# A cross-attention block on one core: an fc pair's weight sums made behind the exchange's copies, batch 1's spread rows loaded later, and batch 3's output projection by seven products of quarter blocks

## The chip, the cores and the metric

The kernel runs on one core of a Trainium2 chip. The metric is the time of one execution on the device in microseconds (us). Engines are called as in the profile: PE multiplies matrices (PEld loads its weights), DVE is the vector engine, ACT the scalar engine, POOL GpSimd, and SP the engine whose queue issues most of the transfers. Each engine works through its own instructions in the order in which they were written, and waits at semaphores for the others.

## The reference, cut to what matters

Four batches of 512 rows by 512 columns, 16 heads of 32 columns, all in float32:

```python
x = layer_norm(hidden_states, ln1_w, ln1_b)
q = (x @ q_w + q_b)...;  k = (enc @ k_w + k_b)...;  v = (enc @ v_w + v_b)...
scores = where(mask, einsum('bhqd,bhkd->bhqk', q, k) / sqrt(32), finfo.min)
out = einsum('bhqk,bhkd->bhqd', softmax(scores), v)
hidden = out @ cproj_w + cproj_b + hidden_states
y = gelu(layer_norm(hidden, ln2_w, ln2_b) @ fc_w + fc_b)     # 512 -> 2048
return hidden + y @ proj_w + proj_b                          # 2048 -> 512
```

The output projection that the change rewrites is `out @ cproj_w` of the last batch.

## The kernel before

**Attention in 32 half-blocks.** Sixteen steps `w` (batch `w // 4`, head group `w % 4` of four heads) have two halves each, so half-blocks p = 0 to 31. `block` computes scores for two query tiles of 128 rows (`scores`, L317), takes minimum and exponential (`soften`, L323 on DVE and L327 on ACT), and turns the probabilities with 32x32 transposes on DVE (`turn`, L335) into a tile `tb`. The exchange (`copies`) then regroups `tb` across partitions into `pT` (for some half-blocks into the free space of `gt` or `xe`): four copies on POOL (L393) for the diagonal pieces and twelve transfers on SP's queue (L398) for the others. `attend` (L415, tiles `av`) multiplies the result with the values and writes `oT`. There is one `pT`, so the next exchange can begin only when `attend` has read the last one. `attend(p - 2)` stands at the start of half-block p from p = 10 on.

**Fill work.** Between the softmax steps PE gets other products: projections of later steps (`acck`, `accq`, `accv`), the output projection of a finished batch (`cproj`, tiles `accc`, L455), and the MLP of batches 0 and 1 (`fc_by_pair`, tiles `q…`, L576; `proj`, tiles `accp`, L636). A table of `put(p, ...)` calls writes by hand which piece stands in which half-block; `some(n)` takes the next n pieces of the MLP list. Nothing is scheduled by a planner: the written order is the order on each engine.

**Seven products.** A pair of fc weight blocks is multiplied with seven products of half-size blocks instead of eight (the Strassen-Winograd scheme). It needs four sums of the weights; `fc_sums` makes them on POOL (`a_sums`, L527 and L530) for up to two pairs ahead, into the two slots of `wsum`, and for batch 0's pairs stores them to `ws` in DRAM with two transfers of POOL's own queue (L619, L620), for batches 2 and 3 to load again (`load_wa`). Before, `fc_sums` is called at the end of `fc_by_pair` and `proj`, right after those have put PE's work in.

**Batch 1's layer norm** comes as rows: `store_rn` writes scale and offset to DRAM, `load_rn` (L213) loads them spread over all partitions (tiles `rn`), `ln1_rows` applies them on POOL (L218), `ln1_affine` on ACT (L222). `load_enc(1)` (L179) brings the next encoder block into `xe`.

**The stretch after the last half-block.** It is written out at the end of `xattn_block`: `attend(15, 0)`, four last pieces of the MLP of batch 1 (`accp_1_0` to `accp_1_3`), `attend(15, 1)`, batch 3's `cproj` for four row tiles, and the weight sums `p_sums`; then `last_mlps` runs the MLPs of the rest, all by seven or 49 products. PSUM has eight banks; `acc_tile` hands them out in turn, four from each of two pools.

```python
run(mlp + norm(2, 2, 3))
p_sums(first_c)
load_wa(first_c + 1)
c = C(B - 1)
run(c[:2])
p_sums(first_c + 2)
run(c[2:])
```

Of the kernel before, what the change touches and what calls it, by code (L numbers as in the profile page):

```python
# [12 lines left out]
F32 = mybir.dt.float32  # L13
# [38 lines left out]
def xattn_block(ctx: ExitStack, tc: tile.TileContext, x, rawT, encT, mask, q_w, k_w, v_w, c_w, fc_w, p_w, vecs, rows, out):  # L52
# [124 lines left out]
    def load_enc(b):  # L177
        for d in range(ND):
            queue(b).dma_start(out=eT[:, d, :], in_=encT[b, ts(d, P), :])  # L179
# [30 lines left out]
    def load_rn(b):  # L210
        S["rows", b] = [hids.tile([P, L], F32, tag="hid2", bufs=2, name=f"rn_{b}_{i}") for i in range(2)]
        for i in range(2):
            nc.sync.dma_start(out=S["rows", b][i], in_=S["rn", b][i : i + 1, :].broadcast_to([P, L]))  # L213

    def ln1_rows(b, *ds):
        for d in ds:
            for i, op in enumerate((ALU.mult, ALU.add)):
                nc.gpsimd.tensor_tensor(S["xn", b][d], S["xn", b][d], S["rows", b][i], op)  # L218

    def ln1_affine(b):  # L220
        for d in range(ND):
            nc.scalar.activation(  # L222
                xT[:, d, :], S["xn", b][d], AF.Identity,
                bias=vec[:, LN1B + d : LN1B + d + 1], scale=vec[:, LN1W + d : LN1W + d + 1],
            )
# [34 lines left out]
    def prep_q(w):  # L260
        b, g = divmod(w, NG)
        qT = k_q(w, 1)
        parts = [slice(0, L)] if w else [slice(0, 2 * P), slice(2 * P, L)]
        for c in parts:
            acc = acc_tile(f"accq_{w}_{c.start}")[:, c]
            for d in range(ND):
                nc.tensor.matmul(acc, S["wq", w][:, d, :], xT[:, d, c], start=(d == 0), stop=(d == ND - 1))  # L267
            nc.scalar.activation(qT[:, c], acc, AF.Identity, bias=qb[:, g : g + 1], scale=-scale)
        load_w(w + 2, names=("wq",))
        S["qT", w] = qT  # L270

    def prep_v(w):
        b = w // NG
        v = five.tile([P, NT, P], F32, tag="v", name=f"v_{w}")
        acc = acc_tile(f"accv_{w}")
        for t in range(NT):
            for d in range(ND):
                nc.tensor.matmul(  # L278
                    acc[:, ts(t, P)], eT[:, d, ts(t, P)], S["wv", w][:, d, :],
                    start=(d == 0), stop=(d == ND - 1),  # L280
                )
        load_w(w + 2, names=("wv",))
        nc.scalar.copy(v, acc.rearrange("p (t f) -> p t f", t=NT))
        S["v", w] = v
        if w:
            v_bias(w)
# [114 lines left out]
    def attend(w, half):  # L401

        b, g = divmod(w, NG)
        if g == 0 and half == 0:
            S["oT", b] = one.tile([P, NG, L], F32, tag="oT", name=f"oT_{b}")
        v, pT = S["v", w], S["pT", w, half]
        av = acc_tile(f"av_{w}_{half}")
        o = S["oT", b][:, g, ts(half, 2 * P)]
        shape, kw = "p (a i q) -> p a i q", dict(a=2, i=NI)
        pv = pT[:, :, :PW].rearrange("p i (a t h q) -> p t h a i q", a=2, t=NT, h=HG)  # L410
        p = [[pv[:, t, h] for h in range(HG)] for t in range(NT)]
        r = pT[:, :, PW:].rearrange("p i (a q) -> p a i q", a=2)
        for t in range(NT):
            for h in range(HG):
                nc.tensor.matmul(  # L415
                    av[ts(h, HD), : 2 * P].rearrange(shape, **kw), v[:, t, ts(h, HD)], p[t][h],
                    start=(t == 0), stop=(t == NT - 1),
                )
        o, a = o.rearrange(shape, **kw), av[:, : 2 * P].rearrange(shape, **kw)
        nc.vector.tensor_tensor(o, a, r, ALU.mult)  # L420
        del held[target(w, half)]
        exchange()
# [28 lines left out]
    def cproj(b, t):  # L451
# [5 lines left out]
        if not stays(b, t):  # L457
            (nc.sync if b == B - 1 else nc.gpsimd).dma_start(out=S["xa", b][ts(t, P), :], in_=h)

    def load_xn(b):  # L460

        for t in range(NT):
            S["h", b, t] = tiles.tile([P, D], F32, tag="xn", name=f"hn_{b}_{t}")
            Q[0].dma_start(out=S["h", b, t], in_=S["xa", b][ts(t, P), :])
# [144 lines left out]
    def fc_sums():  # L609

        while count[3] < len(fc_pairs) and count[3] < count[4] + 2:
            b, c = fc_pairs[count[3]]
            if ("fcw", b, 2 * c + 1) not in S:
                return
            x, y = raw_pair(b, c)
            s = wsum[:, count[3] % 2]
            a_sums(x[:, :2], x[:, 2:], y[:, :2], y[:, 2:], s[:, 0], s[:, 1], y[:, :2], s[:, 2], nc.gpsimd)
            if b == 0:
                nc.gpsimd.dma_start(out=sums_dram[c, :, :3], in_=s)  # L619
                nc.gpsimd.dma_start(out=sums_dram[c, :, 3], in_=y[:, :2])  # L620
            S["ws", b, c] = s[:, 0], s[:, 1], y[:, :2], s[:, 2]
            count[3] += 1

    def fc_by_pair(b, c):
        q, k = divmod(2 * c, FQ)
        fc_seven(b, c, gT[q % 2][:, k : k + 2, :], raw_pair(b, c), S["ws", b, c], acc_half, q % 2)
        count[1] += 2
        count[4] += 1
        load_mlp()
        fc_sums()  # L630

    def proj(b, q, t):
        gelus(q % 2)
        acc = acc_tile(f"accp_{b}_{q}_{t}")
        for k in range(FQ):
            nc.tensor.matmul(  # L636
                acc, gT[q % 2][:, k, ts(t, P)], S["pw", b, q * FQ + k], start=(k == 0), stop=(k == FQ - 1)
            )
        h = S["hid", b, t]
        nc.vector.tensor_tensor(h, acc, h, ALU.add)  # L640
        if q == NQ - 1:
            (nc.gpsimd if b == 0 else nc.sync).dma_start(out=out[b, ts(t, P), :], in_=h)
        count[1] += 1
        load_mlp()
        fc_sums()

# [20 lines left out]
    def last_mlps():  # L669
        last, = pools(ctx, last=1)  # L670
        ps_last = banks.pop()
        assert count[5] % 8 < 4
        count[5] = 0
        ga = last.tile([P, NP, 2, L], F32, tag="ga", name="ga")
        gs = last.tile([P, 3, NP, HL], F32, tag="gs", name="gs")
# [226 lines left out]
    def do(fn):  # L902
        return [(0.0, fn)]

    def next_(fn):
        return [(0.01, fn)]
# [13 lines left out]
    def C(b):  # L920
        return [(CHAIN, lambda t=t: cproj(b, t)) for t in range(NT)]
# [11 lines left out]
    def run(work, budget=None):  # L933

        spent = 0.0
        while work and (budget is None or spent + work[0][0] / 2 <= budget):
            cost, fn = work.pop(0)
            fn()
            spent += cost
        return spent  # L940
# [45 lines left out]
    def some(n):  # L986
        taken = []
        while n > 0:
            n -= 1 if mlp[0][0] == CHAIN else 2
            taken.append(mlp.pop(0))  # L990
        assert n == 0
        return taken
# [4 lines left out]
    def h_(b, *ts_):  # L997
        return do(lambda: load_h(b, *ts_))

    def cb(b):  # L1000
        return do(lambda: c_bias(b))
# [4 lines left out]
    def rs(b):  # L1006
        return do(lambda: ln_rs((2, b)))

    def stat(b, *ts_):
        return do(lambda: [stat2(b, t) for t in ts_])  # L1010
# [6 lines left out]
    def put(p, *work, before=(), mid=()):  # L1017

        work = [item for part in work for item in part]
        ahead[p], mids[p] = list(before), list(mid)  # L1020
        fills[p] = work
# [4 lines left out]
    k5, q5, v5 = A(5)  # L1026
    k6, q6, v6 = A(6)
    put(0, [(CHAIN, lambda: prep_v(1)), v2], do(lambda: store_rn(1)), [k2])
    put(1, [k3, (0.0, lambda: prep_q(1)), (CHAIN, lambda: (prep_v(3), load_enc(1), load_rn(1)))])
    put(2, [q2], [k4], do(lambda: ln1_rows(1, 0, 1)))  # L1030
    put(3, [q3, v4], do(lambda: ln1_rows(1, 2, 3)))
    put(4, [k5, v5], do(lambda: ln1_affine(1)))
    put(5, [q4, q5])
    put(6, [k6, q6])
# [18 lines left out]
        do(lambda: load_rn(3)), some(1))  # L1053

    k, q, v = A(11)
    put(16, do(lambda: ln1_rows(3, *range(ND))), [k, q], some(2))
    put(17, h_(1, 0, 1), next_(lambda: ln1_affine(3)), h_(1, 2, 3), x4, cb(1), C(1))
    k, q, v = A(12)
    put(18, [q], some(2), [k])
    k, q, v = A(13)  # L1060
# [20 lines left out]
    for p in range(2 * NW):  # L1081
        w, half = divmod(p, 2)
        if half == 0 and w and w % NG == 0:
            make_mb(w // NG)
        run(ahead[p])
        for pair in due.get(p, ()):
            attend(*divmod(pair, 2))

        def fill(n, work=fills[p]):
            if n or not work or work[0][0] <= CHAIN:  # L1090
                run(work, CHAIN if n < 2 else None)

        block(w, half, fill, any(cost > CHAIN for cost, _ in fills[p]), mids[p])
# [3 lines left out]
    load_h(B - 1, *range(NT))  # L1097
    run(stat(2, 0, 1))
    attend(NW - 1, 0)
    run(some(2) + stat(2, 2, 3) + rs(2) + cb(B - 1) + norm(2, 0, 1) + some(2))  # L1100
    load_wa(first_c)
    attend(NW - 1, 1)
    run(mlp + norm(2, 2, 3))
    p_sums(first_c)
    load_wa(first_c + 1)
    c = C(B - 1)
    run(c[:2])
    p_sums(first_c + 2)
    run(c[2:])
    att.close()  # L1110
    last_mlps()

# [44 lines left out]
```

## Time and profile before

| | |
|---|---|
| runs | 767.69, 768.56 and 765.34 us, median 767.69 |
| the profiled execution | 765.46 us, of which 763.7 us are its span |
| PE busy | 757.0 us |
| DVE, ACT, POOL busy | 591.2, 336.5 and 329.3 us |
| granted TensorE clock | 1.0 |

A page of the profile shows one execution. Rows of a timeline give the start and the length in microseconds, the engine, the line of the kernel, the operation, and the tiles (output<-input); in brackets stands how long the engine had been idle before it and what ended that. Matmuls of float32 are recorded twice each, so that one written matmul is two records. They overlap by their latency, so the rate of PE is read from start to start, not from a record's length.

### The profile page before, as it was taken

How to read it: one execution, taken by the hardware profiler on the slowest of the kernel's cores; microseconds unless marked ns; L12 is line 12 of the kernel's file. 1: busy time of each engine (PE TensorE's matmuls, PEld its weight loads, DVE VectorE, ACT ScalarE, POOL GpSimd, SP SyncE). 2: the span in 40 equal slices, each digit the busy share in tenths (PEclk: the TensorE clock that was granted, in tenths of full speed). 3: DMA queues.
4: the chain of work that ended last, by engine and by line, in shares of the span. 5: the costliest groups of instructions: out<-in, count | busy, mean ns of one | idle time of the engine just before them, and what ended most of it. 6: DMA issues, size and time to landing. Idle time of an engine off the chain costs nothing.

```text
span 763.7 us, 12836 instructions
## 1 busy us (share of the span) xinstructions
PE 757.0 (99%) x4346; PEld 512.8 (67%) x4346; DVE 591.2 (77%) x1186; ACT 336.5 (44%) x765; POOL 329.3 (43%) x347
## 2 busy tenths in 40 slices
PE   9999999999999999999999999999999999999998
PEld 7655455566574545475454566447888889988997
DVE  3888999879895777887887989855777886747862
ACT  2566766565773574637753567401202221022200
POOL 1538647368564874244575534430050014303152
PEclk9999999999999999999999999999999999999999
DMA  8999879467876686665756867783724402146001
GB/s 328 334 250 243 218 202 258 109 204 210 249 222 212 171 251 198 163 181 125 179 133 186 214 202 187 172 291 131 268 98 135 163 27 90 35 135 217 1 15 42
DMA packets 60576, 134.58 MB, mean 176 GB/s; under 512 B 11312, under 2 KB 17072, under 8 KB 60384
## 3 DMA queue, kind: packets, MB, share of 16 engines
q1 hardware_dynamic: 58448, 126.73, 57.3%
q0 software_dynamic: 1920, 7.01, 2.8%
q8 instruction: 35, 0.57, 0.3%
q14 instruction: 29, 0.24, 0.1%
q10 hardware_dynamic: 144, 0.02, 0.0%
HBM read 69.23 MB, written 11.02 MB: 105 GB/s over the span
## 4 chain that ended last, share of the span: by engine, by line
PE 93%; DMA 4%; SPq 2%; DVE 1%; issue 0%; POOL 0%; POOLq 0%
PE q L576 24%; PE accp L636 11%; PE r L723 8%; PE av L415 8%; PE accc L455 7%; PE sc L317 7%; PE acck L255 7%; PE accq L267 6%; PE accv L278 3%; PE accv L298 3%; PE q4p L759 2%; PE q1p L777 2%; SPq L398 2%; PE tp L166 1%; DMA pbt<-fc_w_dram 1%; DMA ptt<-v_w_dram 1%
## 5 line engine op out<-in xcount | busy, mean ns | idle before, releaser
L327 ACT ACTIVATE ptt<-ptt,mn 128x512 f32<-128x512 f32 x256 | 181.6, 711 | 143.0 <-DVE mn L323 142.9
L323 DVE CUSTOM_DVE_ANT_0 ptt<-sc,mb 128x512 f32<-128x512 f32 x256 | 160.6, 682 | 19.3 <-PE sc L317 19.2
L335 DVE STREAM_TRANSPOSE tb<-ptt 128x1024 f32<-128x1024 f32 x128 | 153.3, 1217 | 0.0
L393 POOL COPY pT<-tb 32x1088 f32<-32x1088 f32 x96 | 104.7, 1090 | 58.8 <-DMA pbt<-p_w_dram 19.0
L636 PE MATMUL accp<-pbt,gt 128*128 128x512 f32 x192 | 84.8, 595 | 0.0
L576 PE MATMUL q<-yT,gt 128*128 128x256 f32 x320 | 78.9, 379 | 0.0
L597 ACT ACTIVATE ga<-ga,vec 128x512 f32<-128x512 f32 x40 | 26.7, 714 | 92.3 <-DVE ga L530 92.3
L576 PEld LDWEIGHTS q<-yT,gt 128*128 128x128 f32 x320 | 60.8, 190 | 8.7 <-issue 0.2
L636 PEld LDWEIGHTS accp<-pbt,gt 128*128 128x128 f32 x192 | 35.9, 190 | 45.1 <-issue 39.9
L317 PE MATMUL sc<-pbt 32*128 32x512 f32 x512 | 65.3, 614 | 0.0
L576 PE MATMUL q<-ys,gt 128*128 128x256 f32 x240 | 61.6, 379 | 0.0
L255 PE MATMUL acck<-xe,ptt 128*128 128x512 f32 x128 | 58.5, 600 | 0.7 <-DVE tb L335 0.7
L267 PE MATMUL accq<-xe,ptt 128*128 128x512 f32 (+1 forms) x136 | 58.5, 574 | 0.0
L455 PE MATMUL accc<-wc,oT 128*128 128x512 f32 x128 | 56.5, 597 | 0.0
L530 DVE TENSOR_TENSOR ga<-q,ga 128x512 f32<-128x512 f32 (+1 forms) x60 | 36.2, 603 | 21.8 <-PE q L576 20.0
L576 PEld LDWEIGHTS q<-ys,gt 128*128 128x128 f32 x240 | 45.6, 190 | 6.2
L327 ACT ACTIVATION_READ_ACCUMULATOR ptt<-ptt,mn 128x1 f32 x256 | 47.8, 187 | 0.0
L415 PE MATMUL av<-pT,v 128*32 128x256 f32 x768 | 46.4, 382 | 1.4 <-DMA pT<-tb 0.7
L267 PEld LDWEIGHTS accq<-xe,ptt 128*128 128x128 f32 x136 | 24.9, 190 | 31.4 <-issue 22.5
L455 PEld LDWEIGHTS accc<-wc,oT 128*128 128x128 f32 x128 | 23.8, 190 | 31.6 <-issue 27.2
L255 PEld LDWEIGHTS acck<-xe,ptt 128*128 128x128 f32 x128 | 23.4, 191 | 31.6 <-issue 22.2
L317 PEld LDWEIGHTS sc<-pbt 32*128 32x128 f32 x512 | 27.3, 183 | 24.9 <-issue 15.8
(190 smaller groups left out, 1228.4 us busy)
## 6 DMA issues: line engine op xcount, KB each, us to landing
pT<-tb SPq DMA_DIRECT2D x288, 136.0 KB, 2.4
pbt<-p_w_dram SPq DMA_DIRECT2D x40, 256.0 KB, 3.8
gt<-ws SPq DMA_DIRECT2D x20, 512.0 KB, 3.4
gt<-tb SPq DMA_DIRECT2D x48, 136.0 KB, 4.3
xe<-tb SPq DMA_DIRECT2D x48, 136.0 KB, 2.8
pbt<-fc_w_dram SPq DMA_DIRECT2D x24, 256.0 KB, 3.5
gt<-fc_w_dram SPq DMA_DIRECT2D x20, 256.0 KB, 3.3
ptt<-k_w_dram SPq DMA_DIRECT2D x16, 256.0 KB, 3.3
```

What stands on the lines that cost most here:

```text
L255: nc.tensor.matmul(acc, S["wk", w][:, d, :], eT[:, d, :], start=(d == 0), stop=(d == ND - 1))
L267: nc.tensor.matmul(acc, S["wq", w][:, d, :], xT[:, d, c], start=(d == 0), stop=(d == ND - 1))
L317: nc.tensor.matmul(S["sc", w, qt][h], qT[r, ts(qt, P)], kT[r, :], start=True, stop=True)
L323: nc.vector.tensor_tensor_reduce(out=s, in0=S["sc", w, qt][h], in1=S["mb", w // NG], scale=1.0, scalar=FMAX, op0=ALU.add, op1=ALU.min, acc ...
L327: nc.scalar.activation(s, s, AF.Exp, bias=mn, scale=-1.0, accum_out=S["sums", w][:, qt, h : h + 1])
L335: nc.vector.transpose(tv[:, qt % 2, 2 * k : 2 * k + 2], S["ps", w, qt, k])
L393: nc.gpsimd.tensor_copy(pT[ts(i, HD), i], tb[ts(i, HD), i])
L415: nc.tensor.matmul(av[ts(h, HD), : 2 * P].rearrange(shape, **kw), v[:, t, ts(h, HD)], p[t][h], start=(t == 0), stop=(t == NT - 1),)
L455: nc.tensor.matmul(acc, S["oT", b][:, g, ts(t, P)], wc[:, g, :], start=(g == 0), stop=(g == NG - 1))
L576: nc.tensor.matmul(o, x[:, k], y[:, k], start=(k == 0), stop=(k == 1))
L636: nc.tensor.matmul(acc, gT[q % 2][:, k, ts(t, P)], S["pw", b, q * FQ + k], start=(k == 0), stop=(k == FQ - 1))
L723: nc.tensor.matmul(r, x[:, c], w[:, c], start=(c == 0), stop=(c == NP // 2 - 1))
```

## The change

It has four parts:

1. `fc_sums` is no longer called in `fc_by_pair` and `proj`, but once in each half-block from p = 11 on, after `attend` (which issues the copies of a waiting exchange) and before `block`. On POOL, an exchange's four copies now stand ahead of the sums that were before them.
2. Batch 1's `load_rn` moves from half-block 1 (right behind `load_enc(1)`) to the end of half-block 2, behind that exchange's transfers; the eight `ln1_rows` operations, before split over half-blocks 2 and 3, all stand in half-block 3.
3. `load_h(1, 0, 1)`, two loads for batch 1's residual, move from half-block 17 to the end of 16, on SP's queue ahead of the twelve transfers of the next exchange.
4. Batch 3's `cproj` becomes `cproj_last`: seven products of quarter blocks, 56 matmul records of 256 columns in place of 32 of 512. Its weight sums (five DVE operations) stand behind `attend(15, 0)`; products 1, 2 and 7 stand among the last MLP pieces; `accp_1_3` stands behind `attend(15, 1)`, then products 6, 3, 5 and 4. The residual is added by three operations on POOL and six on DVE. `norm(2, 2, 3)` moves behind it.

```diff
+    def cproj_last():
...
+        a11, a21, a12, a22 = (S["oT", b][:, 2 * k : 2 * k + 2, ts(i, HL)] for k in range(2) for i in range(2))
+        w11, w12, w21, w22 = (wc[:, 2 * k : 2 * k + 2, ts(j, HL)] for k in range(2) for j in range(2))
+        t1, t2, t4, p1, u2, u3 = (wt[:, n] for n in range(6))
+        s1, s2, s4 = (ot[:, n] for n in range(3))
+        s3, t3 = a21, w12
...
+        def product(n, x, w):
+            q[n] = acc_half(f"q{n}c")
+            for t in range(2):
+                for k in range(2):
+                    nc.tensor.matmul(q[n][:, t], x[:, k, ts(t, P)], w[:, k], start=(k == 0), stop=(k == 1))
+
+        def join(engine, i, j, src):
+            o = h[:, 2 * i : 2 * i + 2, ts(j, HL)]
+            add(engine, o, src, o)
...
+        def one():
+            b_sums(w11, w12, w21, w22, t1, t2, t3, t4)
+            sub(s3, a11, a21)
+
+        def two_():
+            product(1, a11, w11)
+            nc.scalar.copy(p1, q[1])
+            product(2, a12, w21)
+
+        def three():
+            product(7, s3, t3)
+
+        def four():
+            sub(s2, a22, s3)
+            product(6, s2, t2)
+            add(nc.vector, u2, q[6], p1)
+            sub(s4, a12, s2)
+            product(3, s4, w22)
+            add(nc.vector, u3, q[7], u2)
+            add(nc.vector, s1, s2, a11)
+            product(5, s1, t1)
+            join(nc.gpsimd, 1, 0, u3)
+            join(nc.gpsimd, 1, 1, u3)
+            join(nc.gpsimd, 0, 1, u2)
+            join(nc.vector, 0, 0, q[1])
+            join(nc.vector, 0, 0, q[2])
+
+        def five_():
+            product(4, a22, t4)
+            join(nc.vector, 0, 1, q[3])
+            join(nc.vector, 0, 1, q[5])
+            for t in range(2):
+                store(t)
+            join(nc.vector, 1, 1, q[5])
+            join(nc.vector, 1, 0, q[4])
...
     def fc_by_pair(b, c):
...
         load_mlp()
-        fc_sums()
...
     def proj(b, q, t):
...
         load_mlp()
-        fc_sums()
...
-    put(1, [k3, (0.0, lambda: prep_q(1)), (CHAIN, lambda: (prep_v(3), load_enc(1), load_rn(1)))])
-    put(2, [q2], [k4], do(lambda: ln1_rows(1, 0, 1)))
-    put(3, [q3, v4], do(lambda: ln1_rows(1, 2, 3)))
+    put(1, [k3, (0.0, lambda: prep_q(1)), (CHAIN, lambda: (prep_v(3), load_enc(1)))])
+    put(2, [q2], [k4], next_(lambda: load_rn(1)))
+    put(3, [q3, v4], do(lambda: ln1_rows(1, *range(ND))))
...
-    put(16, do(lambda: ln1_rows(3, *range(ND))), [k, q], some(2))
-    put(17, h_(1, 0, 1), next_(lambda: ln1_affine(3)), h_(1, 2, 3), x4, cb(1), C(1))
+    put(16, do(lambda: ln1_rows(3, *range(ND))), [k, q], some(2), h_(1, 0, 1))
+    put(17, next_(lambda: ln1_affine(3)), h_(1, 2, 3), x4, cb(1), C(1))
...
             attend(*divmod(pair, 2))
+        if p > 10:
+            fc_sums()
...
-    run(some(2) + stat(2, 2, 3) + rs(2) + cb(B - 1) + norm(2, 0, 1) + some(2))
+    c = cproj_last()
+    c[0]()
+    run(some(2) + do(c[1]) + stat(2, 2, 3) + rs(2) + cb(B - 1) + norm(2, 0, 1) + some(1) + do(c[2]))
     load_wa(first_c)
     attend(NW - 1, 1)
-    run(mlp + norm(2, 2, 3))
+    run(mlp)
+    c[3]()
     p_sums(first_c)
     load_wa(first_c + 1)
-    c = C(B - 1)
-    run(c[:2])
+    c[4]()
+    run(norm(2, 2, 3))
     p_sums(first_c + 2)
-    run(c[2:])
```

More of the change, by code (lines that the diff above doesn't have):

```diff
@@ L458, in cproj, with store @@
             (nc.sync if b == B - 1 else nc.gpsimd).dma_start(out=S["xa", b][ts(t, P), :], in_=h)
+    def cproj_last():
+        b = B - 1
+        wt, ot = (two.tile([P, NI, PW + 2 * HD], F32, tag="tb", name=n) for n in ("wct", "oTt"))
+        wt, ot = (
+            x.rearrange("p i n -> p (i n)")[:, : 8 * D].rearrange("p (n i f) -> p n i f", n=8, i=2) for x in (wt, ot)
+        )
+        a11, a21, a12, a22 = (S["oT", b][:, 2 * k : 2 * k + 2, ts(i, HL)] for k in range(2) for i in range(2))
[3 more added lines that the diff above has]
+        s3, t3 = a21, w12
+        h = pbt[:, : NT * D].rearrange("p (t n) -> p t n", t=NT)
+        q = {}
+        def product(n, x, w):
[6 more added lines that the diff above has]
+            add(engine, o, src, o)
+        def store(t):
+            nc.sync.dma_start(out=S["xa", b][ts(t, P), :], in_=S["h", b, t])
+        def one():
[29 more added lines that the diff above has]
+            join(nc.vector, 1, 0, q[4])
+            for t in range(2, 4):
+                store(t)
+        return one, two_, three, four, five_
@@ L671, in last_mlps @@
         ps_last = banks.pop()
-        assert count[5] % 8 < 4
         count[5] = 0
```

## The prediction

> **What bounds the kernel now.** I read the page's busy times and its chain first, then the chain of waits in order of time.
>
> ```profile
> PE 757.0 (99%) x4346; PEld 512.8 (67%) x4346; DVE 591.2 (77%) x1186; ACT 336.5 (44%) x765; POOL 329.3 (43%) x347
> PE 93%; DMA 4%; SPq 2%; DVE 1%; issue 0%; POOL 0%; POOLq 0%
> ```
>
> ```profile
> 507.62 13.93 PE accc L455 x32
> 521.55 24.17 PE q L576 x112
> ...
> 760.48 0.02 issue
> ```
>
> PE bounds it: 93% of the chain, and from the end of batch 3's projection (521.55) the chain is PE without a gap up to 760.48. So what moves the start of the first fc pair of `last_mlps` moves the end by as much. Ahead of it only two things pay: less time of PE for the same work, or gaps of PE closed. The timeline of PE has these gaps in the stretches that the change touches:
>
> ```profile
> 52.93 3.67 PE L255 MATMUL acck<-xe,ptt 128*128 128x512 f32 x8 [0.73 <-DVE tb L335]
> ...
> 191.24 1.93 PE L415 MATMUL av<-pT,v 128*32 128x256 f32 x32 [0.41 <-POOL pT L393]
> ...
> 205.09 1.93 PE L415 MATMUL av<-pT,v 128*32 128x256 f32 x32 [0.32 <-DVE gt L530]
> ...
> 219.30 1.93 PE L415 MATMUL av<-pT,v 128*32 128x256 f32 x32 [0.67 <-DMA pT<-tb]
> ...
> 262.70 2.00 PE L317 MATMUL sc<-pbt 32*128 32x512 f32 x16
> 264.62 14.00 PE L455 MATMUL accc<-wc,oT 128*128 128x512 f32 x32
> ...
> 280.42 2.54 PE L317 MATMUL sc<-pbt 32*128 32x512 f32 x16
> 282.89 3.70 PE L267 MATMUL accq<-xe,ptt 128*128 128x512 f32 x8
> ```
>
> The scores at 280.42 have no bracket, but they hold PE until 282.89, 2.47 us, where the same 16 records at 262.70 take 1.92: some 0.54 is a hidden wait. Together 2.67 us.
>
> **Batch 1's rows later.** The first gap stands before keys that read `load_enc(1)`. SP's queue:
>
> ```profile
> 47.37 1.88 SPq L179 DMA_DIRECT2D xe<-encT_dram  x4
> 49.29 0.98 SPq L213 DMA_DIRECT2D rn<-rn  x2
> ```
>
> The four encoder loads are issued ahead of the two that move, on one queue; to take away what stands behind them need not bring them earlier. Bounds 0 and -0.73; I take 0, because of that order. The Trainium skill, "DMA: Bandwidth & Descriptors", section "Queues, rings and completion order", says that each transfer engine consumes its descriptors in ring order: by that rule 0 as well; no row here shows a transfer overtaking another, and if they did share, the sum below would be 0.7 lower.
>
> What the move could cost: all eight `ln1_rows` operations now stand between the value bias and the next copies.
>
> ```profile
> 70.46 5.21 POOL L218 TENSOR_TENSOR raw<-raw,rn 128x512 f32<-128x512 f32 x4
> 75.62 4.47 POOL L393 COPY gt<-tb 32x1088 f32<-32x1088 f32 x4
> ```
>
> ```profile
> 79.97 2.93 ACT L222 ACTIVATE xe<-raw,vec 128x512 f32<-128x512 f32 x4
> ```
>
> ```profile
> 89.42 1.93 PE L415 MATMUL av<-gt,v 128*32 128x256 f32 x32
> ```
>
> Eight from 70.46 at 1.30 each end at 80.9. ACT's fourth activation wants the last at 79.97 + 3 x 0.73 = 82.2; the copies behind them end at 85.4 and PE wants them at 89.42. Cost 0 under those covers of 1.3 and 4 us; without the first, ACT would hold back the next exponentials by what is missing. The two loads are passed by twelve transfers, some 10 us of queue from 49.29, and still come ahead of 70.46.
>
> **Sums behind the copies.** POOL's rows around the second gap, and SP's transfers of that exchange:
>
> ```profile
> 177.35 0.72 POOL L530 TENSOR_TENSOR wsum<-pbt 128x256 f32<-128x256 f32 x1
> ...
> 181.79 4.97 POOL L426 TENSOR_TENSOR h<-h,row 128x512 f32<-128x512 f32 x4
> 186.71 4.48 POOL L393 COPY pT<-tb 32x1088 f32<-32x1088 f32 x4
> ```
>
> ```profile
> 179.80 8.47 SPq L398 DMA_DIRECT2D pT<-tb  x12
> ...
> 207.59 8.65 SPq L398 DMA_DIRECT2D pT<-tb  x12
> ```
>
> ```profile
> pT<-tb SPq DMA_DIRECT2D x288, 136.0 KB, 2.4
> ```
>
> The sums and their two transfers took 177.35 to 181.79. Without them the copies end at 186.8, 4.4 us earlier; the exchange then ends with its transfers, the last issued at about 187.6 and landing 2.4 later, at 190.0, when PE is not free before 190.83. So -0.41 (bounds -0.41 and 0).
>
> The gaps at 205.09 and 219.30 end with transfers: 207.59 + 8.65 = 216.24, and 3.06 later `attend` starts. One `pT` makes a loop of `attend`, twelve transfers, `attend`, which copies that come earlier do not shorten. What changes is POOL's own traffic:
>
> ```profile
> 211.10 0.56 POOL L619 DMA_DIRECT2D ws<-wsum  x1 [0.30 <-POOL wsum L527]
> ```
>
> ```profile
> ws<-wsum POOLq DMA_DIRECT2D x1, 384.0 KB, 3.5
> ws<-pbt POOLq DMA_DIRECT2D x1, 128.0 KB, 4.3
> ```
>
> 512 KB start at 211.10, amid the issues; behind the copies (4.5 us from about 207.2, sums of 3.3 us) they start at about 215, when the last pieces land. Bounds: both gaps gone, -0.99; or, at one of the two places, a writing of 3.5 us wholly ahead of the last landing, of which 3.06 - 2.4 = 0.7 is paid already: +2.8. I take 0: the same bytes cross the same loop, earlier or later.
>
> The sums come later for their users too. The tightest is half-block 30, whose pair is computed in the same half-block:
>
> ```profile
> 460.22 4.47 POOL L393 COPY xe<-tb 32x1088 f32<-32x1088 f32 x4
> ```
>
> ```profile
> 467.55 1.03 PE L576 MATMUL q<-ys,wsum 128*128 128x256 f32 x4
> ```
>
> These copies stood behind the sums that now follow them, so they end by 464.7 at the latest; the third sum (0.75 each) is ready at 466.9, ahead of 467.55. Cost 0, cover 0.6.
>
> **Two loads earlier.** DVE waits for the residual, because POOL's bias for it waits for these loads:
>
> ```profile
> 276.32 0.69 DVE L456 TENSOR_TENSOR h<-accc,h 128x512 f32<-128x512 f32 x1 [5.22 <-POOL h L426]
> ```
>
> ```profile
> 275.03 3.72 POOL L426 TENSOR_TENSOR h<-h,row 128x512 f32<-128x512 f32 x3 [2.45 <-DMA h<-x_dram]
> ```
>
> Issued an exchange earlier, the loads no longer hold POOL: its bias starts 2.45 earlier, and so does DVE's queue of adds, in front of which the scores at 280.42 wait for a bank. -0.54 (bounds -0.54 and 0).
>
> **Batch 3's projection.** Out: 13.93 us. In: 56 records of 128x256 at the pace of the fc pairs, 24.17 / 112 = 0.216: 12.09. That is -1.84. But between the products PE now needs sums of DVE, whose order after `attend(15, 1)` is: add of `accp_1_3`, s2, u2, s4, u3, s1. Its paces:
>
> ```profile
> 509.22 0.68 DVE L527 TENSOR_TENSOR ptt<-pbt 128x512 f32<-128x512 f32 x1
> 509.93 0.69 DVE L527 TENSOR_TENSOR ptt<-pbt,ptt 128x512 f32<-128x512 f32 x1
> 510.54 0.68 DVE L527 TENSOR_TENSOR pbt<-pbt 128x512 f32<-128x512 f32 x1
> ...
> 514.79 0.69 DVE L456 TENSOR_TENSOR pbt<-accc,pbt 128x512 f32<-128x512 f32 x1 [2.37 <-PE accc L455]
> ...
> 552.79 1.77 DVE L527 TENSOR_TENSOR ptt<-pbt,ptt 128x512 f32<-128x512 f32 x1
> ```
>
> An operation takes 0.61 from start to start, 0.71 where the next reads it; it starts 0.2 behind PE's product (the second of the four that begin at 507.62 ends at 514.59).
> - Product 6 reads s2, which stands behind the add of `accp_1_3`, and that waits for PE's product just ahead of 6. PE waits 0.2 + 0.61 + 0.71 = 1.5.
> - Product 3 reads s4, behind u2, which reads product 6: again 1.5.
> - Product 5 reads s1, 1.3 behind s4; product 3 covers it with 1.7.
> - Products 1, 2, 7 and 4 wait for nothing late; the five weight sums lie under `accp_1_0` and `accp_1_1`.
>
> So -1.84 + 3.0 = +1.2. Bounds: -1.84, if both waits were hidden, and +2.3, if one of the sums on this path were stretched to the 1.77 of the row at 552.79 (+1.1).
>
> Behind that, DVE has six adds, eight weight sums and two norms, about 10 us, ahead of the first pair's adds, where before it had one add. It starts on them 1.3 into product 3, has 3.9 until the pair starts (24 records at 0.216, less 1.3) and 2.8 more until the pair's first result (12 records and 0.2), so it comes 3.3 late. PE does not wait for that: eight banks, four to a pair, are used again two pairs or 12 us later, and a pair's four adds take DVE 2.4 of 6.04. Cost 0 under that cover.
>
> **Sum.** 0 - 0.41 + 0 - 0.54 + 1.2 = +0.25 on the profiled execution, 765.46, of which 763.7 is its span (the table above): 765.7. The median of the runs, 767.69, lies 2.2 above it; on the median 767.9.
>
> **Rivals.**
> - A, the waits in the projection do not come, and all gaps close except the first: -1.84 - 1.94 = -3.8, 763.9. For it: the product order puts `accp_1_3` ahead as cover. Against: in DVE's order the add stands ahead of s2.
> - B, slower: POOL's three joins, from u3 on, stretch DVE's sums behind them (at 552.79, beside POOL's adds, 1.77 for 0.68), and DVE's lateness reaches PE. With all nine stretched by 1.1, lateness is 3.3 + 9.9 = 13.2. It decides from about 10, where the third pair finds its bank full, and what the four pairs do not make good comes out before `q1p`, which reads their results:
>
> ```profile
> 521.39:545.56 24.17, 14.66 (x26) 1.00 0.58 202
> ```
>
> That is the four pairs' stretch, and DVE's busy time in it. It has 24.17 - 14.66 = 9.5 free, some 2.2 of it ahead of the first result, so 13.2 - 7.3 = 5.9 is left: +5.9 + 0.25, 773.8. Against it: three joins of 1.25 last 3.7, so two or three sums are stretched. The Trainium skill, "SBUF — State Buffer", section "Who interferes with whom", says that a vector instruction with two SBUF inputs and a GpSimd one that reads SBUF shut each other out for the whole instruction. The row at 552.79 agrees.
> - C, POOL's writes delay the exchanges: +2.8 + 0.25, 770.7. For it, the start at 215; against it, half of each write is done by then.
> - D, the moves change no gap and only the projection counts: +1.2, 768.9.
>
> **Numbers.** Forecast 60%, D 15%, A 13%, C 6%, B 6%. Predicted 767.9. The runs shown lie 2.4 below and 0.9 above their median. The range, 764.8 to 770.8, takes in D and C and most of the way to A, and leaves B out. A measurement of this kernel can tell about 0.5%, 3.8 us, from no change: faster by more needs A and more, 6%; slower by more needs B, or C with a slow measurement, 10%; within it 84%.
>
> **What would show it.** PE waiting for DVE ahead of products 6 and 3, 1.5 each, right; no such waits, wrong, and A. The gap at 191 gone; those at 205 and 219 still there; the scores at 280 back at 1.93; the gap at 52.9 unchanged. The first fc pair of `last_mlps` starting about 0.3 later than 521.55, and no gap behind it; a gap in the third pair would be B. Wrong altogether: a gap of over 1 us at a place that I gave cost 0.

## The result, and the profile after

| | before | after |
|---|---|---|
| median of the runs | 766.24 us (6 runs, 765.34 to 768.56) | 770.86 us (6 runs, 768.58 to 772.72) |
| ratio, with its 95% interval | | 1.0053 (1.003 to 1.0076) |
| profiled execution, its span | 765.46, 763.7 us | 768.58, 766.7 us |

The forecast was 767.9, the range ended at 770.8. The kernel became 4.1 us slower by the ratio (2.3 to 5.8); its profiled execution, the shortest of its runs, 3.0 by the span, where the sum had +0.25. The page still names PE as the bound (its busy times, and the chain that ended last):

```profile
PE 755.5 (99%) x4370; PEld 516.3 (67%) x4370; DVE 601.4 (78%) x1198; ACT 337.3 (44%) x766; POOL 335.1 (44%) x350
PE 96%; DVE 2%; DMA 1%; SPq 0%; issue 0%; POOL 0%; DVEq 0%; POOLq 0%
```

PE has 1.5 us less of work, and 4.5 us more in which it does nothing. Where, the timeline of PE shows (changed kernel; start, length, operation, idle time before it):

```profile
52.49 2.97 PE L255 MATMUL acck<-xe,ptt 128*128 128x512 f32 x6 [0.38 <-issue]
56.03 1.12 PE L255 MATMUL acck<-xe,ptt 128*128 128x512 f32 x2 [0.58 <-DMA gt<-tb]
57.09 1.93 PE L415 MATMUL av<-pT,v 128*32 128x256 f32 x32
...
191.32 1.93 PE L415 MATMUL av<-pT,v 128*32 128x256 f32 x32
...
207.64 1.93 PE L415 MATMUL av<-pT,v 128*32 128x256 f32 x32 [2.78 <-DVE gt L598]
...
221.11 1.93 PE L415 MATMUL av<-pT,v 128*32 128x256 f32 x32
...
282.23 2.00 PE L317 MATMUL sc<-pbt 32*128 32x512 f32 x16
284.23 3.67 PE L267 MATMUL accq<-xe,ptt 128*128 128x512 f32 x8
...
515.69 1.99 PE L479 MATMUL q6c<-wct,oTt 128*128 128x256 f32 x8 [1.38 <-DVE oTt L595]
519.14 1.99 PE L479 MATMUL q3c<-wc,oTt 128*128 128x256 f32 x8 [1.45 <-DVE oTt L595]
...
524.42 1.89 PE L644 MATMUL q<-yT,gt 128*128 128x256 f32 x8
```

Two of the rows before:

```profile
56.53 1.93 PE L415 MATMUL av<-pT,v 128*32 128x256 f32 x32
...
521.39 1.89 PE L576 MATMUL q<-yT,gt 128*128 128x256 f32 x8
```

Each row is set against the row of the same work before; the difference of the starts is the lateness at that point, and its steps are what each stretch cost:

| the work | before | after | lateness | step |
|---|---|---|---|---|
| `attend` behind batch 1's keys | 56.53 | 57.09 | +0.56 | +0.56 |
| `attend` near 191 | 191.24 | 191.32 | +0.08 | -0.48 |
| `attend` near 205 | 205.09 | 207.64 | +2.55 | +2.47 |
| `attend` near 219 | 219.30 | 221.11 | +1.81 | -0.74 |
| the work behind the scores at 280 | 282.89 | 284.23 | +1.34 | -0.47 |
| first fc pair of `last_mlps` | 521.39 | 524.42 | +3.03 | +1.69 |

From 524.42 on nothing is gained or lost. So the steps for the gap at 191 and for the scores hold, and two gaps moved that were to stay, one of them with the largest loss: 2.47 at `attend` near 205. The trace names DVE's `gt` there:

```profile
204.94 1.95 DVE L598 TENSOR_TENSOR gt<-q,gt 128x512 f32<-128x512 f32 x3
```

The last of these three operations ended at 206.89, and before at 206.81, when PE had started at 205.09 already. So `attend` doesn't wait for it. What it waits for, by the experiments below, is the last pieces of the exchange. SP's twelve transfers and POOL's writes around it, changed kernel:

```profile
191.84 2.22 SPq L184 DMA_DIRECT2D xn<-x_dram  x4
194.15 10.11 SPq L398 DMA_DIRECT2D pT<-tb  x12
```

```profile
190.73 0.56 POOL L687 DMA_DIRECT2D ws<-wsum  x1 [0.30 <-POOL wsum L595]
...
201.76 0.56 POOL L687 DMA_DIRECT2D ws<-wsum  x1 [0.30 <-POOL wsum L595]
```

The same exchange before, and the one write that fell into it:

```profile
193.75 9.15 SPq L398 DMA_DIRECT2D pT<-tb  x12
194.60 0.56 POOL L619 DMA_DIRECT2D ws<-wsum  x1 [0.30 <-POOL wsum L527]
```

Before, the writes of these two pairs (the third and the fourth) were issued at 180.67, in the exchange before, and at 194.60, 0.85 behind this exchange's first transfer. Now one stands ahead of the exchange's 1 MB of `xn` loads, the other 7.6 behind the first transfer.

The medians lie 4.6 us apart and the profiled executions 3.0, so 1.6 us are not in this timeline. Of the six runs, the two shortest (768.58 and 769.59) had a mean granted clock of 1.0, the other four (770.78 to 772.72) one of 0.996 to 0.998. What lowers it shows in the profiles of e2, e4 and e6 below; that the same happened in these four runs is likely, but no profile of them shows it.

### The profile page after: what moved, and what is told of

Same layout as the page of the kernel before. It is cut to its first block, busy times and chain, and to the rows that moved or that the text cites. A ratio compares the mean times of both kernels' runs of the same rounds, so it can differ in the third digit from the quotient of the medians.

```text
span 766.7 us, 12899 instructions
## 1 busy us (share of the span) xinstructions
PE 755.5 (99%) x4370; PEld 516.3 (67%) x4370; DVE 601.4 (78%) x1198; ACT 337.3 (44%) x766; POOL 335.1 (44%) x350
## 4 chain that ended last, share of the span: by engine, by line
PE 96%; DVE 2%; DMA 1%; SPq 0%; issue 0%; POOL 0%; DVEq 0%; POOLq 0%
PE q L644 25%; PE accp L703 11%; PE r L788 8%; PE sc L317 8%; PE av L415 8%; PE accq L267 7%; PE acck L255 7%; PE accc L455 6%; PE accv L278 5%; PE accv L298 3%; PE q4p L824 2%; PE q1p L842 2%; PE tp L166 1%; DMA gt<-tb 1%; DVE ptt L323 1%; PE warm L1021 1%
## 5 line engine op out<-in xcount | busy, mean ns | idle before, releaser
L455 PE MATMUL accc<-wc,oT 128*128 128x512 f32 x96 | 42.5, 598 | 0.0
L415 PEld LDWEIGHTS av<-pT,v 128*32 128x32 f32 x768 | 22.7, 109 | 26.9 <-issue 11.0
```

What stands on the lines that cost most here:

```text
L415: nc.tensor.matmul(av[ts(h, HD), : 2 * P].rearrange(shape, **kw), v[:, t, ts(h, HD)], p[t][h], start=(t == 0), stop=(t == NT - 1),)
L455: nc.tensor.matmul(acc, S["oT", b][:, g, ts(t, P)], wc[:, g, :], start=(g == 0), stop=(g == NG - 1))
```

## The experiments

The ratios are to runs of the kernel before on the same chip; microseconds are (ratio - 1) x 766.4.

**The parts by themselves.** e1 is the kernel before with part 4, e2 with part 1, e3 with parts 2 and 3, each as in the diff above. e4 is the changed kernel with three of DVE's sums moved:

```diff
+        def sums():
+            sub(s2, a22, s3)
+            sub(s4, a12, s2)
+            add(nc.vector, s1, s2, a11)
         def four():
-            sub(s2, a22, s3)
...
-            sub(s4, a12, s2)
...
-            add(nc.vector, s1, s2, a11)
...
     attend(NW - 1, 1)
+    c[5]()
     run(mlp)
```

> The kernel before with the seven products for batch 3's projection alone (part 4). My theory, from the two traces: PE waits for DVE ahead of products 6 and 3 (1.4 us idle each in the changed kernel's profile), so the first fc pair of the last MLPs starts 1.7 us later after the scores of the last half-block than before, and the time is 1.7 us above the kernel before, with no other gap changed. Rival: the waits belong to other parts of the change (late DVE work from the moved sums); then the projection is 1.8 us shorter and the time falls by that.

> The kernel before with the weight sums behind the exchange's copies alone (part 1). My theory: two writes of POOL's queue (512 KB each, at about 191 and 202) now fall between the issue of half-block 12's twelve transfers and their landing or just ahead, where one did, so attend after half-block 13 waits 2.8 us (0.3 before); the gaps at 191 and at 219 (0.4 and 0.7) close; together the time is 1.5 us above the kernel before. Rival: the 2.8 us come from the changed start of batch 1's rows or from chance of that execution; then that gap stays at 0.3 and the time falls by 0.4 to 1.1.

> The kernel before with parts 2 and 3 alone: batch 1's spread rows loaded later, and batch 1's two residual loads earlier. My theory: PE loses 0.5 us in the keys at 52 (the exchange's transfers, issued 1.5 us earlier, share the transfer engines with the encoder loads, whose landing goes from 6.0 to 7.0 us) and gains 0.5 us at the scores behind batch 1's projection (280); the time is that of the kernel before within 0.3. Rival by ring order: the encoder loads don't land later, the keys lose nothing, and the time falls by 0.5.

> The changed kernel with only DVE's order in the last stretch altered: s2, s4 and s1 stand right behind attend(15, 1), ahead of the add of accp_1_3, and u2 and u3 behind them. My theory: both waits came from what DVE had ahead of s2 and s4, so both go; PE runs products 6, 3, 5 and 4 without a gap, the first fc pair starts 2.8 us earlier, and the time is 2.8 us under the changed kernel, about that of the kernel before. Rival: the waits are for the products themselves (PE's latency and the banks), then at most 1 us of the 2.8 is gained.

| | ratio (95%) | us |
|---|---|---|
| e1, projection alone | 1.0026 (1.0014 to 1.0038) | +2.0 |
| e2, sums alone | 1.0045 (1.0028 to 1.0062) | +3.4 |
| e3, both loads alone | 0.9993 (0.9981 to 1.0004) | -0.5 |
| e4, change with DVE's order mended | 1.0016 (1.0002 to 1.003) | +1.2 |

The parts add to 4.9, the change has 4.1. e1 shows the same two waits (1.38 and 1.45), so they belong to part 4. In e4 both are gone. First the changed kernel's DVE in the last stretch, then e4's:

```profile
510.74 0.42 DVE L420 TENSOR_TENSOR oT<-av,xe 128x256 f32<-128x256 f32 x1 [2.93 <-PE av L415]
514.35 0.69 DVE L707 TENSOR_TENSOR hid<-accp,hid 128x512 f32<-128x512 f32 x1 [3.18 <-PE accp L703]
514.95 0.68 DVE L595 TENSOR_TENSOR oTt<-oT 128x512 f32<-128x512 f32 x1
517.79 0.69 DVE L598 TENSOR_TENSOR wct<-q6c,wct 128x512 f32<-128x512 f32 x1 [2.16 <-PE q6c L479]
518.40 0.68 DVE L595 TENSOR_TENSOR oTt<-oT,oTt 128x512 f32<-128x512 f32 x1
```

```profile
514.19 0.42 DVE L420 TENSOR_TENSOR oT<-av,xe 128x256 f32<-128x256 f32 x1 [2.93 <-PE av L415]
514.65 0.69 DVE L597 TENSOR_TENSOR oTt<-oT 128x512 f32<-128x512 f32 x1
515.37 0.69 DVE L597 TENSOR_TENSOR oTt<-oT,oTt 128x512 f32<-128x512 f32 x1
515.98 0.68 DVE L600 TENSOR_TENSOR oTt<-oTt,oT 128x512 f32<-128x512 f32 x1
517.79 0.69 DVE L709 TENSOR_TENSOR hid<-accp,hid 128x512 f32<-128x512 f32 x1 [1.12 <-PE accp L705]
```

In the changed kernel DVE idles 3.18 us ahead of the add of `accp_1_3` while s2 (the `oTt` at 514.95) has had its inputs since 511.2, and idles 2.16 ahead of u2 (`wct` at 517.79) while s4 (518.40) is ready to run. In e4 the three sums fill the first of these holes, and PE runs the products without a gap:

```profile
514.05 3.70 PE L705 MATMUL accp<-pbt,gt 128*128 128x512 f32 x8
517.59 1.89 PE L479 MATMUL q6c<-wct,oTt 128*128 128x256 f32 x8
519.32 1.89 PE L479 MATMUL q3c<-wc,oTt 128*128 128x256 f32 x8
...
524.50 1.89 PE L646 MATMUL q<-yT,gt 128*128 128x256 f32 x8
```

From the start of `accp_1_3` to the first fc pair it takes 10.45 us, the changed kernel 524.42 - 510.61 = 13.81: 3.36 less. That is the two waits from start to start: product 6 begins 515.69 - (510.61 + 8 x 0.4325) = 1.62 late, product 3 519.14 - (515.69 + 8 x 0.216) = 1.72. In the runs e4 is 2.9 under the change, where 2.8 was expected.

e2 cost 3.4 where 1.5 was expected, and its timeline says why:

```profile
207.95 2.57 PE L415 MATMUL av<-pT,v 128*32 128x256 f32 x32 [3.70 <-DMA ptt<-k_w_dram]
210.45 3.00 PE L317 MATMUL sc<-pbt 32*128 32x512 f32 x16
```

The gap near 205 is 3.70 in place of 2.78, and the work *behind* it is slow: `attend` takes 2.57 where 1.93 is usual, the scores 3.00 for 2.00. The windows of e2 (length, PE busy, granted clock, share of the DMA engines, GB/s) show the clock:

```profile
207.00:209.00 2.00, 1.05 (x20) 1.00 0.85 307
209.00:211.00 2.00, 2.00 (x23) 0.52 0.13 47
211.00:213.00 2.00, 2.00 (x16) 0.62 0.41 94
213.00:215.00 2.00, 2.00 (x12) 1.00 0.96 220
```

Half the clock for some 3 us, 1.6 us lost. In the changed kernel's profile, with a gap of 2.78, the same windows read 1.00 throughout. In e4's profile, with 3.65, four windows read 0.50 to 0.75, and `attend` and the scores took 2.7 us more. The Trainium skill, "TensorE: Matmul & The Clock Gate", section "What's actually happening", says that the array's clock falls to half once a free-running window of about 3.4 us has passed idle, and comes back after a busy one. The rows agree in the main: no fall at 2.78, one at 3.20 (e6, below), 3.65 and 3.70; 3.20 is a little under the page's window, and there the measurement decides. So half a microsecond more of a gap can cost 1.6 to 2.7 us on top of the gap. That this parts the changed kernel's runs is inferred from their mean clocks.

e3 came out at -0.5 (-1.5 to +0.3), which fits both theories. Its profile shows the two pieces apart: the scores at 280 at 2.0 us, and the keys near 52 late as in the change.

**Which write delays the exchange.** Four kernels. e5 and e6 start from e4: e5 issues the fourth pair's write one half-block later; e6 makes the sums of the first three pairs where they were before the change; e8 leaves parts 1 and 2 out (part 3, and part 4 with DVE's order of e4); e9 is e8 with the fourth pair's write alone issued behind the copies.

```diff
     def fc_sums():
+        for o, i in late:
+            nc.gpsimd.dma_start(out=o, in_=i)
+        late.clear()
...
-            if b == 0:
+            if b == 0 and c == 3:
+                late.extend([(sums_dram[c, :, :3], s), (sums_dram[c, :, 3], y[:, :2])])
+            elif b == 0:
```

```diff
-    def fc_sums():
+    def fc_sums(to=len(fc_pairs)):
...
         load_mlp()
+        fc_sums(3)
```

The first of these is e5, the second e6. e9 has e5's list `late`, but empties it in the loop over the half-blocks:

```diff
             attend(*divmod(pair, 2))
+        for o, i in late:
+            nc.gpsimd.dma_start(out=o, in_=i)
+        late.clear()
```

> The kernel of e4 (the change with DVE's order in the last stretch mended), and the write of the fourth pair's sums alone issued one half-block later, behind the copies of half-block 13's exchange. In the change that write is issued at 201.8 and 202.3, amid the last transfers of half-block 12's exchange, which already follow the third pair's write (190.7) and 1.5 MB of loads. Theory 1, two writes to one exchange: attend after half-block 13 waits 0.5 us or less in place of 2.8 to 3.7, the clock stays at 1.0 behind it, attend after half-block 14 waits some 0.7, and the time is 3 us under that of e4 and the kernel before. Theory 2, a write late in an exchange costs its whole length: the gap moves to attend after half-block 14 (near 219), 2 us or more, and the time stays that of e4. Theory 3, the third pair's write ahead of the exchange's loads is what costs: the gap near 205 stays over 1.5 us.

> The kernel of e4, and the sums of the first three pairs (0 to 2) made at the places of the kernel before, the others at those of the change. So the third pair's write goes back from 190.7 to about 181, into the exchange before, and the fourth pair's stays at 202. Theory 1 (two writes to one exchange): the gap near 205 falls to 1 us or less, the gap of 0.4 at 191 comes back, and the time is 2.5 us under e4. Theory 2 (the late write costs its length): the gap near 205 stays at 2 us or more.

> The kernel before with part 3 and with part 4 with DVE's order mended; parts 1 and 2 left as before. From e3 and e4: the residual loads earlier give 0.5, the projection 1.8 (32 records of 512 columns for 56 of 256), no gap changes elsewhere: 2.3 us under the kernel before. Rival: the products' waits turn up elsewhere (DVE's work in the last stretch is longer), and less than 1 us is left.

> The kernel of e8 with one edit: the fourth pair's sums stay where they were before the change (191 to 194 on POOL), only their write (512 KB) is issued behind the copies of half-block 12's exchange, at about 200.2 in place of 194.5. Theory 2 (a write that falls amid the last transfers of an exchange costs nearly its whole length): attend after half-block 13 waits 2 to 3 us near 205 in place of 0.45, and where the idle time passes some 3.2 us the granted clock falls to 0.5 behind it; time 2 to 4 us over e8. Rival (the sums' own place on POOL, or the third pair's write, makes the gap): it stays under 1 us and the time is that of e8.

| | writes, us behind the exchange's first transfer | idle at `attend` near 205 | ratio (95%) | us |
|---|---|---|---|---|
| e8 | +0.85 | 0.45 | 0.998 (0.9971 to 0.999) | -1.5 |
| e9 | +4.5 | 0.98 | 0.9981 (0.997 to 0.9992) | -1.5 |
| e5 | -3.3 | 1.82 | 0.9997 (0.9984 to 1.0009) | -0.2 |
| e6 | +7.9 | 3.20 | 1.0013 (0.9999 to 1.0027) | +1.0 |
| the change | -3.4 and +7.6 | 2.78 | 1.0053 | +4.1 |
| e4 | -3.5 and +7.5 | 3.65 | 1.0016 | +1.2 |

PE's row in e6, where the trace names the exchange's pieces:

```profile
207.95 2.58 PE L415 MATMUL av<-pT,v 128*32 128x256 f32 x32 [3.20 <-DMA pT<-tb]
```

Each idle time is that of one execution. In the six profiles with the write at its old place (before, e1, e3, e8, e10 and e11) this gap is 0 to 0.88, so only differences beyond that can be read.

Theory 1 (two writes to one exchange) falls: e6 has one and waits as long as two. Theory 2 (a late write costs its length) holds in e6; Theory 3 holds for the other write, which by itself gives 1.82 in e5. The runs agree: by the ratios, e5 is 1.3 and e6 2.5 above e8, which also lacks part 2. Taken together the two writes don't add. POOL's copies are not what PE waits for: in e6 they end at 198.2, in e8 at 200.0.

e9 was to be the clean test of the late write, and missed its place: with the write no longer ahead of them, the copies began 1.3 us earlier, and the write came out at +4.5, not +6.6. Its gap, 0.98, is what the rival expected, and hardly above the 0.88 without a move of the write. So by e8's row the write cost some 0.5 at +4.5, no more than that scatter, and some 2.8 at +7.9.

Why late costs more than early, though the bytes are the same, can be read from the windows of e8 and e6 (the last two numbers are the share of the DMA engines and GB/s):

```profile
196.00:200.00 4.00, 4.00 (x14) 1.00 0.95 316
200.00:204.00 4.00, 4.00 (x20) 1.00 0.96 255
204.00:207.00 3.00, 2.55 (x39) 1.00 0.80 274
```

```profile
196.00:200.00 4.00, 4.00 (x14) 1.00 0.95 200
200.00:204.00 4.00, 4.00 (x21) 1.00 0.83 205
204.00:207.00 3.00, 0.75 (x4) 1.00 0.94 295
```

The exchange's pieces alone keep the engines busy by their share, but move only 200 GB/s; with the write among them it is 316. An early write rides along (116 GB/s x 4 us = 0.46 MB, close to the write's 0.52). In e6 that room is left empty, and the write shares the engines with the last pieces, for which PE waits. This reading is worked out from the windows; no run took the pieces' form itself as its variable.

e6 also shows the clock once more. Its twelve runs fall into five with a mean clock of 1.0, 764.86 to 767.12 us, and seven with 0.998 or 0.999, 767.62 to 769.47.

e8 expected -2.3 and had -1.5, the -2.3 just outside its interval (-2.2 to -0.8); its span, 761.3, is 2.4 under that of before. The difference stays open.

**What stands behind the encoder loads.** e7 was to put the load of the value weights between the encoder loads and the exchange:

```diff
-(CHAIN, lambda: (prep_v(3), load_enc(1)))
+(CHAIN, lambda: (load_enc(1), prep_v(3)))
```

> The kernel before with parts 2, 3 and 4, DVE's order mended in part 4, and in half-block 1 the four encoder loads issued ahead of the load of the value weights. Theory (transfers behind the encoder loads share the engines with them, so what stands behind them matters): the value weights take the place of the exchange's pieces, the encoder loads start 0.4 us earlier, and the keys at 52 wait 0.3 us or less in all, where they lose 1.5 with part 2 and 0.9 without; time 3 us under the kernel before. Rival by ring order: only the earlier start counts, the keys wait 0.5 less than with part 2, time 2.3 under.

It took 773.67 us, a ratio of 1.0105 (1.0091 to 1.012), and tells nothing of this: `prep_v(3)` holds the value *products* too, which then read the encoder tile behind batch 1's loads (so batch 0's last values come from batch 1's rows), and PE idled 7.33 us ahead of them. The question went to the landing times instead. Every profile lists the four loads, with the time from issue to landing; it has a landing for the last two of them only, which are the least and the greatest below:

```profile
L179 SPq DMA_DIRECT2D xe<-encT_dram x4: 420/428/462, 47.4 to 48.8; - x4
...
DMA to landing us min/median/max: 5.9/6.0/6.1
```

```profile
L179 SPq DMA_DIRECT2D xe<-encT_dram x4: 420/427/530, 47.0 to 48.4; - x4
...
DMA to landing us min/median/max: 6.4/7.0/7.6
```

The first is the kernel before, the second the change. In the six profiles without part 2 the fourth load takes 0.1 to 0.3 longer than the third, in the six with it 0.7 to 1.2. By the means, the third goes from 5.6 to 6.2 and the fourth from 5.8 to 7.2. In e7, whose exchange begins only 10 us behind the loads, both take 5.4. The fourth decides: in the change PE's last two records of the keys wait until 56.03, which is 48.4 + 7.6. So what is issued behind the loads does hold them up, the last one most. For PE it is little: from the scores near 46.5 to `attend`, 9.0 to 10.2 us without part 2 (mean 9.8) and 9.4 to 10.9 with it (mean 10.3).

**The change mended.** e10 is e8, with the sums from the fifth pair on behind the copies, the first four at their old places. e11 is e10 with part 2: the whole change, mended in two places. (`fc_sums` has e6's argument `to`.)

```diff
         load_mlp()
-        fc_sums()
+        fc_sums(4)
...
             attend(*divmod(pair, 2))
+        if p > 10:
+            fc_sums()
```

> The kernel of e8, with the sums of the first four pairs where they were before the change, and those from the fifth on behind the exchange's copies as the change has them. Theory: the gap near 205 stays that of e8 (0.45), the fifth pair's write moves from 211 to 218, behind the last transfers of half-block 13's exchange, so the gap near 219 (0.4 to 0.7) closes as it did in the change; time 0.4 to 0.7 us under e8, some 2.3 under the kernel before. Rival: the write at 218 delays the loads and the exchange that come next, and a new gap of over 0.7 us opens at attend near 233 or at the scores behind; time that of e8 or above.

> The whole change, mended in two places: DVE's order in the last stretch as in e4, and the sums of the first four pairs at their old places as in e10. It differs from e10 by part 2 alone (batch 1's spread rows loaded later). Theory (the exchange's pieces that follow the encoder loads at once share the engines with them): the four encoder loads land 1 us apart in latency (6.4 to 7.6 us in the change, 5.9 to 6.1 before), and from the scores at 46.5 to attend PE needs 10.3 us where it needs 9.9 without part 2; time 0.3 us over e10, some 2.8 under the kernel before. Rival by ring order: the four latencies are equal, and the time is that of e10 or 0.5 under it.

e10: 763.78 us, ratio 0.9959 (0.9942 to 0.9975), -3.1 us. e11: 764.26 us, ratio 0.9971 (0.9955 to 0.9986), -2.2 us. Both beat the kernel before, by 0.4% and 0.3%, and the change. e10 has the lowest ratio; that it is faster than e8 isn't shown, as its profiled span is 761.9 and that of e8 761.3. Its three places, and the transfers of the third:

```profile
192.05 1.93 PE L415 MATMUL av<-pT,v 128*32 128x256 f32 x32 [0.46 <-POOL pT L393]
205.96 1.93 PE L415 MATMUL av<-pT,v 128*32 128x256 f32 x32 [0.37 <-DVE gt L600]
219.42 1.93 PE L415 MATMUL av<-pT,v 128*32 128x256 f32 x32
```

```profile
208.46 8.01 SPq L398 DMA_DIRECT2D pT<-tb  x12
...
216.38 0.56 POOL L689 DMA_DIRECT2D ws<-wsum  x1 [0.30 <-POOL wsum L597]
```

The gap near 219 is closed, with a write at +7.9 too; but here the twelve transfers are issued by 216.47, so the write comes when the last is already out. In e6, behind 1.5 MB of loads, they took 10.18, and 2.3 us of issues were still to come behind the write. So the time behind the first transfer doesn't decide by itself. By the reading above it is what the write meets: early it rides along (e9, with 3.8 us of issues still to come), with the last piece out it delays nothing that shows (e10), and in between it shares the engines with the last pieces (e6). But the exchanges of e6 and e10 also differ in the loads ahead of them, and no run holds the one and varies the other. e11's landing times are 6.7/7.2/7.6, as expected of part 2, and its stretch of keys 10.75 us against e10's 10.15; that part 2 costs time can't be told from the runs, as the two intervals overlap.

## Why the prediction was right or wrong

The measured median, 770.86, lies 0.06 above the end of the range (764.8 to 770.8), and the direction, slower, is that of the forecast; its size is not, 4.1 us for 0.2. That the time came so near the range is in part luck: the forecast was built on a median before of 767.69, and six runs gave 766.24, so the range stood 1.45 too high. In the mechanism the prediction was wrong at one step above all, the gap near 205, and its own sign of being wrong altogether came there: a gap of over 1 us, 2.78, at a place that was given cost 0.

- **Batch 1's rows later, taken as 0:** +0.56 in the profile, some 0.5 by the mean of the profiles with and without, and not told from 0 by the runs' times. The step that failed here is that order on the queue protects the loads ahead. The rule of the Trainium skill that it leaned on, "DMA: Bandwidth & Descriptors", section "Queues, rings and completion order", that each engine consumes descriptors in ring order, was read for more than it says: the same paragraph adds that a later descriptor may finish its write before an earlier one. Here the load that decides landed 1.4 us later, by the means. The rows that I quoted for the price of the move were of POOL, ACT and PE, none of what the exchange does to the loads when it starts 1.5 us earlier. POOL's and ACT's covers held.
- **The gap at 191, -0.41:** right (-0.48).
- **The gap near 205, taken as 0 within -0.99 and +2.8:** +2.47, and 1.6 to 2.7 more in executions where the clock falls. This is the step that made the forecast wrong, and it was rival C's mechanism, given 6%. It failed in two ways. The argument "the same bytes cross the same loop, earlier or later" isn't so: into this exchange, the write cost nothing that shows at +0.85 and 2.8 us at +7.9, and the third pair's write ahead of it gave 1.82 by itself. And I worked the timing out for one exchange, that of 207.59, which starts with little ahead of it, and carried it to the one before it, which follows 1.5 MB of loads and which two writes moved towards. The upper bound lacked the clock, for which the trace of before, with no gap above 0.73 behind its start, has no row.
- **The gap at 219, taken as 0:** -0.74; it was called unchanged, and it closed: no gap in the change, nor in e2, e4, e6, e10 and e11, in which the fifth pair's write alone stands behind these copies, where before, e1, e3, e8 and e9, without that move, have 0.25 to 1.65. In e5, which adds the fourth pair's write there, it is 0.80.
- **The loads for the residual, -0.54:** right (-0.47).
- **The projection, -1.84 + 3.0 = +1.2:** the mechanism right in each step, the two waits 1.62 and 1.72 rather than 1.5 each, and 0.2 more that isn't assigned: +1.69. e4 shows both causes that were named, the add ahead of s2 and u2 ahead of s4. Without them the stretch takes 10.45, where its 8 records of `accp_1_3` and 32 of the products add up to 10.37.
- **DVE's lateness at no cost:** right. Two weight sums beside POOL's joins took 1.66 and 1.64 in place of 0.68, and the first pair's add started at 532.02, some 4.8 us after the pair's first result where 3.3 was said; PE had no gap behind. That is rival B's mechanism, below the point from which it decides.

Of the signs that were named, the waits ahead of products 6 and 3, the gap at 191, the scores at 280 and the absence of a gap behind the first fc pair came as said. The pair was 3.0 late and not 0.3, and the gaps at 52.9, 205 and 219 did not stay.

## What to carry to other kernels

Before a bulk write is moved, look at what else is on the transfer engines at its new place, exchange by exchange: here the same 512 KB write was nearly free early in an exchange, cost 2.8 us late in it, and nothing that shows in another exchange whose last piece was out. When products need sums made between them, write into the vector engine's order first the sums whose inputs are ready, then whatever waits for the matrix engine. Price a gap of the matrix engine that may grow past some 3 us (2.78 brought no fall here, 3.20 did) at itself and the clock's fall behind it.

## What the runs showed that was not expected

- A gap of PE of 3.2 to 3.7 us was followed by a granted clock of about 0.5 for 3 to 6 us, 1.6 to 2.7 us of time; 2.78 was not. The runs of e6 part by the mean clock, as said above; those of e4 less clearly: two of the six runs at 0.995 to 0.997 lie among those at full clock.
- With an exchange's transfers issued right behind four loads on the same queue, the third load landed 0.6 and the fourth 1.4 us later after its issue than with two other loads between, by the means of six and six profiles.
- From 196 to 200 us the transfer engines moved 200 GB/s in e6, with the 136 KB pieces on 32 partitions and no write beside them, and 316 in e8, with the 512 KB write beside them; their busy share was 0.95 in both.
